# Attention with a second, small attention on one Trainium2 core: the masks of the token keys move ahead of most weight sums in the setup, and in the last batch the spreading of the probabilities and the bias move ahead

## The chip, the cores and the metric

The kernel runs on one core of one Trainium2 chip. The core has five engines that run side by side and meet through semaphores: the matrix engine (PE, which loads weights, PEld, and multiplies), VectorE (DVE), ScalarE (ACT), GpSimd (POOL) and SyncE (SP), which here issues nearly all DMAs. Each engine carries out its own instructions in the order in which the program gives them. The metric is the time on the device in microseconds (us); a profile is one execution recorded by the hardware.

## The reference

There are 16 batches of 100 rows of 640 (`hidden_states`), and for each batch 722 context rows of 384. The last four context rows are the tokens `ca`, the first 718 are `enc`. All is in float32, with eight heads of 80.

```python
query = hidden_states @ Wq;  keyt = enc @ Wk;  valt = enc @ Wv
hs = _mha(query, keyt, valt)
ca_q1 = jnp.einsum('btc,th->bch', ca, Wq_ca)[:, indices, :]   # 100 of 384 channels
ca_hs1 = _mha(ca_q1, residual, residual)
ca_q2 = ca_hs1 @ Wq
ca_hs2 = _mha(ca_q2, ca @ Wk_ca, ca @ Wv_ca)                  # four keys
out = (hs + ca_hs2) @ Wout + b_out + residual
```

`_mha` is softmax attention with the factor 80 to the power of -0.5.

## The kernel before, in words

The order of all instructions is written out by hand, engine by engine; nothing plans it. The kernel has a setup, a loop over the 16 batches, and a last projection.

**The products with the context.** The 3 x 2 blocks of the value product (three chunks of the 384 context channels, two halves of the 640 columns, three thirds of the context rows) are computed with 15 block products in place of 18, and those of the first four chunks of keys likewise. For that, sums of blocks of the weights are formed once (`weight_sums`, L511, one DVE instruction for each of twelve sums, at L531, for `wv_sb` and for `wk_sb` each), and sums of blocks of the context for each batch (`enc_sums`, L486, on POOL, L507). `weight_sums(engine, w, late, part)` goes through the list of twelve, of which `part` takes a slice; with `late` True or False it takes only those of the five forms (5, 7, 13, 3, 14) or only the others. Form 7 needs form 5, and 13 and 3 need 7. The block products of a batch and the copies and sums that move them out of PSUM are issued piece by piece by `vv.go(n)` (values, L439, moved at L410 and L412) and `kk.go(n)` (the next batch's keys, L470).

**The setup.** Seven idle products (L1257), then the first batch's keys (`first_keys`, L597). DVE forms the weight sums as the weights land. PE computes the keys of all tokens into `k2_ps` (L1289); DVE multiplies them by a mask of the heads, once for each of the five chunks of 128 columns (`k2T`, L1301; in the profile its tile bears the name `wq`, because it lies in a spare part of a tile of that name). With the masked keys PE computes `m` in five groups (`m_ps`, L1313), each of five products with the transposed Wq. DVE copies each group out (L1321), SP writes it to DRAM (L1325), and DVE forms one weight sum. POOL spreads `m` into `m2` for a batch (`keys`, L766, at L771); ACT copies Wq into place (L1272, L1280).

Then `Second`, the small attention of a batch: `products` (`y_ps`, L799; DVE reduces it into `g`, L808), `scores1` (`e1`, L834 and L841, for the first batch on DVE, for the others on POOL), `softmax1` (a maximum over blocks and its subtraction, L723 to L753 and L851, DVE), `exponentials1` (ACT, L854), and `softmax2` (`z_ps`, L861). `scores2` and `softmax3` give the probabilities of the four tokens: POOL writes them into `p2_in` (L900).

**A batch.** PE computes scores (`s_ps`, L660), ACT copies them into three tiles `st`, DVE takes the maximum over keys (L1399, L1408, and the class `Maximum`), subtracts it (`subtract`, L1387), and ACT takes the exponential (L1395). Then PE computes the rows' remaining columns and sums (`r_ps`, L1537) and the weighted values (`a_ps`, L1555). `divide` (L1025) takes the reciprocal of the sums on DVE and sends it through DRAM into `ratio` (SP, L1035 and L1038). `spread2` (L907) transposes the token probabilities on DVE (L910), writes them to DRAM with four DMAs (L913), copies them there in a wider layout (L918) and loads them back, spread over the partitions, with three more (L923, L927). `values2` (L929) then multiplies them by the token values on POOL, seven instructions (L937, L941), into `hs2`. `add_bias` (L1009) adds the bias to the loaded residual rows on POOL (L1015).

**The last batch** (L1491 to L1515) has no next batch to prepare. Two of its three subtractions are done by POOL, behind the first one on DVE. Behind them POOL has `values2` and then `add_bias`. DVE combines values, ratio and `hs2` for the last rows (`finish`, L1082, at L1086 and L1092, first chunk 4, then chunks 0 and 1, then 2 and 3), PE projects them (`project_last`, L1208, at L1219, in the order of chunks 4, 0, 1, and then 2 and 3), DVE adds the residual (L1228) and SP stores them (L1231).

Of the kernel before, what the change touches and what calls it, by code (L numbers as in the profile page):

```python
# [59 lines left out]
for h in range(NH):  # L60
    lo = h * D
    while lo < (h + 1) * D:
        c = lo // P
# [84 lines left out]
def kernel(  # L148
# [18 lines left out]
    nc = tc.nc  # L167
# [76 lines left out]
    def load_enc(b):  # L244
        enc = enc_tile(f"enc_{b}"), None
        for u, lo, hi in ((0, 0, 3), (1, 1, 3), (2, 0, 2)):
            at = A_RAW[u, lo]
            nc.sync.dma_start(
                out=enc[0][:, at : at + hi - lo],
                in_=enct[b][:, lo:hi, u * (KT - 1) : u * (KT - 1) + KT],  # L250
            )
        return enc

    def load_rest(b, enc):
        if b == 1:
            room = hsT_tile("rest_1").rearrange("p c s -> p (c s)")
            rest = room[:, : len(A_REST) * KT].rearrange("p (i k) -> p i k", k=KT)
        else:
            rest = rest_tile(f"rest_{b}")
        for (u, c), i in A_REST.items():  # L260
            nc.sync.dma_start(
                out=rest[:, i], in_=enct[b][:, c, u * (KT - 1) : u * (KT - 1) + KT]
            )
        return enc[0], rest
# [9 lines left out]
    wv_sb = const.tile([P, NF, H // 2], F32, name="wv_sb")  # L274
    wk_sb = const.tile([P, NF, 2, P], F32, name="wk_sb")
# [210 lines left out]
    def enc_sums(enc, part=slice(None)):  # L486

        at = lambda f: a_form(enc, f)
        raw = lambda u, c: a_raw(enc, u - 1, c - 1)
        sums = (  # L490
            (at(7), raw(2, 3), raw(3, 1), ALU.add),
            (at(11), raw(3, 2), raw(3, 3), ALU.add),
            (at(8), at(11), raw(2, 3), ALU.subtract),
            (at(10), raw(1, 3), at(11), ALU.subtract),
            (at(9), raw(2, 1), raw(2, 2), ALU.add),
            (at(2), raw(1, 1), at(9), ALU.subtract),
            (at(9), at(9), raw(3, 1), ALU.subtract),
            (at(5), raw(1, 1), raw(2, 1), ALU.subtract),
            (at(5), at(5), raw(2, 3), ALU.add),
            (at(11), raw(1, 3), raw(3, 3), ALU.subtract),  # L500
            (at(11), at(11), raw(3, 1), ALU.add),
            (at(4), at(2), at(10), ALU.add),
            (at(4), at(4), raw(1, 2), ALU.add),
        )
        begun = None
        for out, left, right, op in sums[part]:
            first = nc.gpsimd.tensor_tensor(out, left, right, op)  # L507
            begun = begun or first
        return begun

    def weight_sums(engine, w, late=None, part=slice(None)):  # L511

        at = lambda f: w[:, W_AT[f]]
        raw = lambda c, g: w[:, 2 * (c - 1) + g - 1]
        sums = (
            (0, raw(1, 2), raw(1, 1)),
            (11, raw(2, 2), raw(3, 2)),
            (12, raw(3, 2), raw(3, 1)),
            (5, raw(2, 2), raw(1, 2)),
            (7, raw(3, 2), at(5)),  # L520
            (13, raw(3, 1), at(7)),
            (1, raw(2, 1), raw(3, 1)),
            (3, raw(1, 1), at(7)),
            (6, raw(2, 1), raw(1, 1)),
            (10, raw(3, 1), raw(2, 2)),
            (2, raw(1, 1), raw(2, 2)),
            (14, raw(2, 1), raw(2, 2)),
        )
        for f, left, right in sums[part]:
            if late is None or late == (f in (5, 7, 13, 3, 14)):  # L530
                engine.tensor_tensor(at(f), left, right, ALU.subtract)  # L531
# [731 lines left out]
    nc.gpsimd.memset(most[96:, :], LOW)  # L1263
    nc.gpsimd.memset(e1[96:, :], LOW)
    weight_sums(nc.vector, wk_sb, False)
    weight_sums(nc.vector, wv_sb, part=slice(6))
    weight_sums(nc.vector, wk_sb, True)
    enc_sums(enc)

    for c in range(HC):  # L1270
        for u in range(2):
# [25 lines left out]
    for n, heads in enumerate(HEADS):  # L1297
        cols = len(heads) * B * T
        k2T.append(room[:, at : at + cols])
        at += cols  # L1300
        nc.vector.tensor_tensor(  # L1301
            k2T[n].rearrange("p (h k) -> p h k", h=len(heads)),
            k2_ps[:, n * B * T : (n + 1) * B * T]
            .unsqueeze(1)
            .to_broadcast([P, len(heads), B * T]),
            hmask[:, n, : len(heads)].unsqueeze(2).to_broadcast([P, len(heads), B * T]),
            ALU.mult,
        )
    enc_next = load_rest(1, load_enc(1))
    for c in range(HC):  # L1310
        m_ps = psum(f"m_ps_{c}")
        for n, heads in enumerate(HEADS):
            nc.tensor.matmul(  # L1313
                m_ps[:, heads[0] * B * T : (heads[-1] + 1) * B * T],
                wqt_sb[:, n, c * P : (c + 1) * P],
                k2T[n],
                start=(n == 0),
                stop=(n == HC - 1),
                skip_group_check=True,
            )  # L1320
        nc.vector.tensor_copy(  # L1321
            m_sb[c].rearrange("p (b h t) -> p h b t", h=NH, t=T),
            m_ps.rearrange("p (h b t) -> p h b t", h=NH, b=B),
        )
        nc.sync.dma_start(out=m_d[c], in_=m_sb[c])  # L1325
        weight_sums(nc.vector, wv_sb, part=slice(6 + c, 7 + c))
    weight_sums(nc.vector, wv_sb, part=slice(11, None))
    nc.sync.dma_start(out=wvca_sb, in_=wvca.rearrange("(c p) n -> p c n", p=P))
    second = Second(0, xT, ca_0)
    keys(load_m(0))  # L1330
# [37 lines left out]
    last, late, second_next = None, False, Second(1, xT)  # L1368
    for b in range(B):
        p = b // 2  # L1370
        e_in, now = enc, second
        enc, second = enc_next, second_next
        mine = Last(b)
# [51 lines left out]
        if b + 1 < B:  # L1425

            def both(n):
                vv.go(n)
                kk.go(n)

            if waiting:
                wait_for(enc_sums(enc, LATE_SUMS), seen)
            if waiting:
                second.scores1(tokens=range(T - 1))
            else:
                second.scores1(seen)
            store(seen)
            if last:
                last.load(seen)
            if b == B - 2:  # L1440
                again()
            if b + 2 < B:
                m_next = load_m(b + 2, seen)
            if b == 1:
                load_outputs(nc.sync.dma_start, wout_sb, wout)
            top.go(3)
            both(3)
            now.scores2()
            top.go(1)
            both(2)  # L1450
            top.go()
            both(2)
            now.softmax3()
            if waiting:
                second.scores1(tokens=range(T - 1, T))
            if b + 2 < B:
                keys(m_next)
            both(1)
            now.spread2()
            vv.go(2)  # L1460
            kk.go(1)
            subtract(0)
            exponential(0)
            vv.go(1)
            less = subtract(1)
            if last:
                last.place(less)
                if last.b in PAIRED:
                    last.row_sums()
                last.add_bias()  # L1470
            if b == B - 2:
                mine.load(seen)
            now.values2()
            if b == B - 2:
                mine.add_bias()
            vv.go(1)
            kk.go(2)
            exponential(1)
            vv.go(1)
            kk.go(2)  # L1480
            both(1)
            both(1)
            if b == 1:
                nc.gpsimd.dma_start(out=bias, in_=bout[0].partition_broadcast(P))
            second_next, enc_next = loads()
            subtract(2)
            exponential(2)
            last_keys(b + 1, enc)
            if b + 2 < B:
                enc_next = load_rest(b + 2, enc_next)  # L1490
        else:  # L1491
            last.place()
            mine.load(seen)
            top.go(3)
            vv.go(3)
            top.go(1)
            now.scores2()
            last.project_few(len(OC) - 2)
            last.project((0,), True, put=False)
            top.go()  # L1500
            now.softmax3()
            vv.go(2)
            less = subtract(0)
            exponential(0)
            wait_for(subtract(2, nc.gpsimd), less)
            subtract(1, nc.gpsimd)
            now.spread2()
            now.values2()
            mine.add_bias()
            vv.go(5)  # L1510
            exponential(2)
            vv.go(1)
            exponential(1)
            vv.go(4)
            last.put()  # L1515
        paired = last and last.b in PAIRED
        late = b % 2 == 0 and not paired
# [107 lines left out]
```

## Time and profile before

| | us |
|---|---|
| median of 3 runs | 927.84 (927.64 to 929.23) |
| the profiled execution | 925.61 |
| its span | 923.9 |
| mean granted PE clock | 0.998 |
| PE busy | 913.9 |
| DVE busy | 668.9 |
| POOL busy | 622.6 |
| ACT busy | 376.7 |

The profile's page gives the busy time of each engine; a row of its timeline is start, duration, engine, line, operation, the tile written and the tiles read, shapes and count, and in brackets how long the engine was idle before and whose work ended that. `PE` is the multiplying, `PEld` the loading of weights, and a letter q behind an engine's name its queue. The granted clock is the share of full speed at which PE ran.

### The profile page before, as it was taken

Reading aid. Unit: us, or ns where it says so; the run is one execution under the profiler, and the core shown is the slowest. Engines: PE = TensorE matmul, PEld = TensorE weight load, DVE = VectorE, ACT = ScalarE, POOL = GpSimd, SP = SyncE. Lnnn points to the kernel's source line nnn. Section 1 sums busy time; section 2 is a strip of 40 time slices with the busy share of each in tenths; the row PEclk is TensorE's granted clock in tenths of the full one; section 3 lists DMA queues with packets and bytes.
Section 4 is the critical chain, followed back from the end, with each engine's and each line's share of the span. In section 5 each row is a group of like instructions: output and inputs, shape, how many; then the busy total and the mean of one; then the engine's idle time right before and its main releaser. Section 6 shows DMA issues by size and latency. Waiting matters only on the chain.

```text
span 923.9 us, 26078 instructions
## 1 busy us (share of the span) xinstructions
PE 913.9 (99%) x11155; PEld 778.7 (84%) x11155; DVE 668.9 (72%) x1121; ACT 376.7 (41%) x654; POOL 622.6 (67%) x653
## 2 busy tenths in 40 slices
PE   9999999999999999999999999999999999999997
PEld 8988889797887979888798788988888888887965
DVE  4799695978639796675957759488782878729783
ACT  2253533444325443433434334344542435424441
POOL 9555787587946788476674756856695576945644
PEclk9999999999999999999999999999999999999999
DMA  9604251051402403140221403205140151401312
GB/s 293 207 13 131 52 131 39 15 133 34 109 12 57 118 15 100 43 131 12 70 74 43 131 13 87 65 5 135 41 109 11 35 141 34 110 12 46 84 45 71
DMA packets 68060, 69.50 MB, mean 75 GB/s; under 512 B 25192, under 2 KB 61352, under 8 KB 67944
## 3 DMA queue, kind: packets, MB, share of 16 engines
q1 hardware_dynamic: 67016, 66.97, 27.0%
q8 instruction: 88, 1.44, 0.6%
q10 hardware_dynamic: 464, 0.52, 0.2%
q0 software_dynamic: 464, 0.34, 0.2%
q14 instruction: 28, 0.23, 0.1%
HBM read 62.14 MB, written 8.94 MB: 77 GB/s over the span
## 4 chain that ended last, share of the span: by engine, by line
PE 92%; DMA 3%; DVE 2%; POOL 1%; ACT 1%; issue 0%; SPq 0%; POOLq 0%; ACTq 0%; DVEq 0%
PE s_ps L660 12%; PE v_psA L439 11%; PE v_psB L439 9%; PE k_psA L470 8%; PE q_ps L544 7%; PE a_ps L1555 7%; PE k_psB L470 7%; PE kT_ps L568 6%; PE r_ps L1537 4%; PE v_psC L439 3%; PE k_psC L470 3%; PE y_ps L799 2%; PE o_psy L1128 2%; PE v_psE L439 2%; PE v_psD L439 2%; PE k_psE L470 1%
## 5 line engine op out<-in xcount | busy, mean ns | idle before, releaser
L834 POOL TENSOR_TENSOR e<-ca,g 100x800 f32<-100x800 f32 x60 | 91.8, 1540 | 101.8 <-DVE most L1399 75.2
L439 PE MATMUL v_psA<-wv_sb,enc 128*120 128x320 f32 x384 | 119.5, 434 | 0.0
L507 POOL TENSOR_TENSOR enc<-enc 128x240 f32<-128x240 f32 x144 | 111.1, 781 | 8.0
L439 PE MATMUL v_psB<-wv_sb,enc 128*120 128x320 f32 x320 | 99.2, 432 | 0.0
L660 PE MATMUL s_ps<-qp,kT 32*120 32x100 f32 x3072 | 97.4, 263 | 0.0
L660 PEld LDWEIGHTS s_ps<-qp,kT 32*120 32x120 f32 x3072 | 94.7, 179 | 1.9
L841 POOL TENSOR_TENSOR e<-e,e 100x800 f32<-100x800 f32 x45 | 92.1, 2047 | 3.5
L439 PEld LDWEIGHTS v_psA<-wv_sb,enc 128*120 128x120 f32 x384 | 69.0, 183 | 24.7 <-DVE vs L410 0.9
L1387 DVE TENSOR_TENSOR st<-st,over 120x1600 f32<-120x1600 f32 x46 | 88.7, 1929 | 0.0
L470 PE MATMUL k_psA<-enc,wk_sb 128*128 128x240 f32 x360 | 87.6, 366 | 0.0
L470 PEld LDWEIGHTS k_psA<-enc,wk_sb 128*128 128x128 f32 x360 | 68.4, 190 | 17.1
L1399 DVE TENSOR_TENSOR most<-most,st 120x800 f32<-120x800 f32 x64 | 63.9, 998 | 23.3 <-ACT st L682 22.2
L439 PEld LDWEIGHTS v_psB<-wv_sb,enc 128*120 128x120 f32 x320 | 58.6, 183 | 23.4
L1395 ACT ACTIVATE st<-st 120x1600 f32<-120x1600 f32 x48 | 73.9, 1540 | 7.6 <-DVE st L1387 5.2
L470 PE MATMUL k_psB<-enc,wk_sb 128*128 128x240 f32 x300 | 73.0, 366 | 0.0
L1408 DVE TENSOR_TENSOR most<-st 120x800 f32<-120x800 f32 x16 | 16.5, 1032 | 75.9 <-ACT st L688 75.9
L1555 PE MATMUL a_ps<-st,vs 120*64 120x100 f32 (+1 forms) x1536 | 69.5, 250 | 0.0
L544 PE MATMUL q_ps<-xT,wq_sb 128*128 128x200 f32 x400 | 69.1, 332 | 0.0
L1555 PEld LDWEIGHTS a_ps<-st,vs 120*64 120x64 f32 (+1 forms) x1536 | 66.4, 137 | 2.7 <-issue 2.7
L544 PEld LDWEIGHTS q_ps<-xT,wq_sb 128*128 128x128 f32 x400 | 68.0, 190 | 0.2
L688 ACT COPY st<-s_ps 120x800 f32<-120x800 f32 x64 | 49.7, 829 | 43.4 <-PE s_ps L660 43.4
L412 ACT COPY vs<-v_psA 120x640 f32<-120x640 f32 x48 | 33.3, 693 | 83.7 <-PE v_psA L439 83.7
(183 smaller groups left out, 1893.1 us busy)
## 6 DMA issues: line engine op xcount, KB each, us to landing
pb<-p_d SPq DMA_DIRECT2D x32, 400.0 KB
enc<-in_enct SPq DMA_DIRECT2D x30, 240.0 KB
enc<-in_enct SPq DMA_DIRECT2D x15, 360.0 KB
xT<-in_xt SPq DMA_DIRECT2D x8, 500.0 KB
rest<-in_enct SPq DMA_DIRECT2D x31, 120.0 KB
xn<-in_x SPq DMA_DIRECT2D x11, 320.0 KB
wide_d<-p_d SPq DMA_DIRECT2D x16, 200.0 KB
pb<-wide_d SPq DMA_DIRECT2D x16, 200.0 KB
```

The source lines that it names most:

```text
L439: nc.tensor.matmul(at[0][j][:KN, : H // 2], a_form(self.enc, f)[:, j * KN : (j + 1) * KN], wv_sb[:, W_AT[f]], start=first, stop=last, skip ...
L470: nc.tensor.matmul(at[:, i * KT : (i + 1) * KT], wk_sb[:, W_AT[f], i], a_form(self.enc, f), start=(first and i == 0), stop=last, skip_grou ...
L507: first = nc.gpsimd.tensor_tensor(out, left, right, op)
L544: nc.tensor.matmul(q_ps[:, : 2 * S].rearrange("p (j s) -> p j s", j=2), wq_sb[:, c, n * P : (n + 1) * P], xT[:, :, c, :], start=(c == 0), ...
L568: nc.tensor.matmul(bank[:, i * KT : (i + 1) * KT], weights[c], a_raw(enc, u, c), start=(i == 0 and c == 0), stop=(c == CC - 1), skip_group ...
L660: nc.tensor.matmul(s_ps[bank][:n, 256 * a + lo : 256 * a + lo + rhs.shape[-1]], kT[rows, c, u, j * KN : (j + 1) * KN], rhs, start=bank not ...
L834: first = engine.tensor_tensor(to, self.ca[:, t, :].unsqueeze(1).to_broadcast([S, NH, S]), g[:, :, t].unsqueeze(2).to_broadcast([S, NH, S] ...
L841: engine.tensor_tensor(e, e, to, ALU.add)
L1387: return engine.tensor_tensor(st[i], st[i], top.over[:KN].unsqueeze(1).to_broadcast([KN, 2, ROWS]), ALU.subtract,)
L1395: nc.scalar.activation(st[i], st[i], AF.Exp, scale=SCALE)
L1399: most_now = nc.vector.tensor_tensor(most[:KN], most[:KN], st[i][:, u], ALU.max)
L1555: nc.tensor.matmul(wides[64 * e : 64 * e + 64, h // 2], slot(i, h, FIRST[e], 64), st[i // 2][: KEYS[i], i % 2, h * S : (h + 1) * S], start ...
```

## The change

In the setup DVE's order becomes: the seven early sums of `wk_sb`, four sums of `wv_sb` (six before), and then at once the five masks `k2T`. All five late sums of `wk_sb`, which stood ahead of the masks, and the last eight of `wv_sb` go into a list, in the order wk 5, 7, 13, 3, then eight of wv, then wk 14 (thirteen in all). Two of them are issued between the masks and m's loop, one behind each of m's five copies, and six behind the loop. (Before, one sum of wv stood behind each copy and one behind the loop.)

In the last batch `spread2` moves ahead of the second of the two block sums that stood ahead of it, and ahead of the three subtractions; `add_bias` moves ahead of `values2`. The number of instructions stays the same.

```diff
     weight_sums(nc.vector, wk_sb, False)
-    weight_sums(nc.vector, wv_sb, part=slice(6))
-    weight_sums(nc.vector, wk_sb, True)
+    weight_sums(nc.vector, wv_sb, part=slice(4))
     enc_sums(enc)
+    gaps = [(wk_sb, True, slice(k, k + 1)) for k in (3, 4, 5, 7)]
+    gaps += [(wv_sb, None, slice(k, k + 1)) for k in range(4, 12)]
+    gaps += [(wk_sb, True, slice(11, None))]
+
+    def fill(n):
+        for w, late, part in gaps[:n]:
+            weight_sums(nc.vector, w, late, part)
+        del gaps[:n]
...
+    fill(2)
     enc_next = load_rest(1, load_enc(1))
     for c in range(HC):
         m_ps = psum(f"m_ps_{c}")
...
         nc.sync.dma_start(out=m_d[c], in_=m_sb[c])
-        weight_sums(nc.vector, wv_sb, part=slice(6 + c, 7 + c))
-    weight_sums(nc.vector, wv_sb, part=slice(11, None))
+        fill(1)
+    fill(len(gaps))
...
             now.softmax3()
-            vv.go(2)
+            vv.go(1)
+            now.spread2()
+            vv.go(1)
             less = subtract(0)
             exponential(0)
             wait_for(subtract(2, nc.gpsimd), less)
             subtract(1, nc.gpsimd)
-            now.spread2()
+            mine.add_bias()
             now.values2()
-            mine.add_bias()
             vv.go(5)
```

## The prediction

> **What bounds the kernel now.** I read the page first, then every wait of the matrix engine, then the timeline around the two long ones, and the windows view for the clock.
>
> ```profile
> span 923.9 us, 26078 instructions
> PE 913.9 (99%) x11155; PEld 778.7 (84%) x11155; DVE 668.9 (72%) x1121; ACT 376.7 (41%) x654; POOL 622.6 (67%) x653
> ```
>
> PE is busy for 99% of the span, so time can only come out of PE's idle time or out of a slower PE clock. Its waits over the whole span, as total, count and longest (the two smallest left out):
>
> ```profile
> PE o_ps L1219 <- DVE spare L1092: 2.2, 1, 2.2
> PE m_ps L1313 <- DVE wq L1301: 1.8, 1, 1.8
> PE idle_ps L1257 <- DVE vaT L1254: 1.1, 1, 1.1
> PE z_ps L861 <- issue: 0.4, 1, 0.4
> PE k_ps L1289 <- ACT kT L631: 0.2, 1, 0.2
> PE z_ps L861 <- ACT e L854: 0.2, 1, 0.2
> ...
> ```
>
> The two largest are exactly where the diff works: m's products wait for the masked token keys (L1301), and the last projection waits for the last sum on DVE (L1092). Between them PE waits 0.6 us (two z_ps waits), so what is gained in the setup should arrive at the end.
>
> **Part 1, the setup.** Timeline of before (start, duration, engine, line):
>
> ```profile
> 17.85 5.01 DVE L531 TENSOR_TENSOR wv_sb<-wv_sb 128x320 f32<-128x320 f32 x6 [5.09 <-DMA wv_sb<-in_wv]
> 22.52 1.97 PE L1289 MATMUL k_ps<-beside,tokens 128*64 128x64 f32 x60 [0.24 <-ACT kT L631]
> 22.73 2.50 SPq L248 DMA_DIRECT2D enc<-in_enct  x3
> 22.78 3.27 DVE L531 TENSOR_TENSOR wk_sb<-wk_sb 128x256 f32<-128x256 f32 x5
> 25.98 1.20 DVE L1301 TENSOR_TENSOR wq<-k_ps,hmask 128x128 f32<-128x128 f32 x5
> 26.31 8.56 PE L1313 MATMUL m_ps<-wq,wout_sb 128*128 128x128 f32 x50 [1.82 <-DVE wq L1301]
> 29.37 0.29 ACT L1280 COPY wq_sb<-wq 128x128 f32<-128x128 f32 x1
> 32.27 0.69 DVE L1321 COPY m<-m_ps 128x512 f32<-128x512 f32 x1 [0.23 <-PE m_ps L1313]
> ...
> 34.91 0.69 DVE L1321 COPY m<-m_ps 128x512 f32<-128x512 f32 x1 [0.23 <-PE m_ps L1313]
> 35.51 0.98 DVE L531 TENSOR_TENSOR wv_sb<-wv_sb 128x320 f32<-128x320 f32 x2
> 37.56 0.26 DVE L808 TENSOR_REDUCE g<-y_ps 100x32 f32<-100x96 f32 x1 [1.07 <-PE y_ps L799]
> 53.92 0.99 DVE L851 TENSOR_TENSOR e<-e,over 100x800 f32<-100x800 f32 x1
> 56.56 0.90 ACT L854 ACTIVATE e<-e 100x800 f32<-100x800 f32 x1
> ```
>
> PE has the token keys at 22.52 + 1.97 = 24.49. DVE masks them only at 25.98, because eleven weight sums stand ahead of the masks. The change leaves four of these (17.85 + 4 x 5.01 / 6 = 21.2), so DVE reaches the masks long before 24.49 and waits for PE instead. Nothing is queued behind that wait that anyone needs earlier. The mask of chunk n needs only chunk n's columns: m's first product started 0.33 after the first of five masks began, so slices are followed one by one on this side, and I take it that they are on the other. Then m starts right behind the token keys, at about 24.5, and the 1.82 us go. The other end: if the first mask waits for all token keys, m starts 0.33 after 24.49 and 1.5 go. I take 1.8. No weight sum is added or removed, only moved.
>
> There is a second cost behind this gap. Windows of before (us, busy of PE, PEld, DVE, ACT, POOL, then the granted clock, DMA share, GB/s):
>
> ```profile
> 23.45:26.87 3.42, 1.59 (x40) 1.46 (x37) 3.28 (x9) 1.97 (x7) 1.57 (x2) 1.00 1.06 363
> 26.87:30.28 3.41, 3.41 (x15) 3.41 (x15) 1.40 (x4) 2.52 (x9) 0.47 (x1) 0.50 1.02 298
> 30.28:33.70 3.42, 3.42 (x28) 3.42 (x27) 2.29 (x5) 0.00 (x0) 1.00 (x2) 1.00 0.47 175
> 910.84:914.25 3.41, 1.57 (x38) 1.37 (x32) 1.30 (x1) 0.00 (x0) 3.33 (x3) 1.00 0.27 81
> ```
>
> Right after the stretch with the gap, PE was granted half its clock for 3.41 us: 15 matmuls in place of 28. That cost 3.41 x 0.5 = 1.7 us. The copies confirm it: the copies at 32.27 and 34.91 stand two groups of m apart, so a group takes 1.32; five would be 6.6, and m took 8.56, 1.96 more. The page's forty slices hide this. I take it that the gap caused it and that it goes too: 1.7. The other end is 0, since the last row, a stretch of the tail with as little PE work, was not followed by a low clock.
>
> The Trainium skill, page "TensorE: Matmul & The Clock Gate", Part 1 on the clock gate, says that the clock halves after about one whole idle window of roughly 3.4 us and that the windows run freely. The length of the low stretch agrees; the cause does not, for the gap was 1.82. By that rule this gap could not have lowered the clock, so the low stretch would have another cause, and could come again; that is the first rival.
>
> What is late next? Shift the setup by 3.5. The query weights are copied by 29.37 + 0.29 = 29.66, and the first queries then start at 26.31 + 8.56 - 3.5 = 31.4: covered. SP's issue at 22.73 waited for the landing of the transposed Wq that m reads (SP's waits name that transfer), so m's weights are there before 24.5. Two wk sums now stand between masks and m's first copy, 2 x 3.27 / 5 = 1.3 at most against 1.32 of PE for one group; within the loop a copy and a sum (0.69 + 0.49) fit into 1.32. Behind the last copy, six sums stand in place of two: 6 x 0.49 = 2.9, from 34.91 + 0.69 - 3.5 = 32.1 to 35.0. The first batch's g (L808) could start at 34.06 and so is 0.9 late against its shifted place. From g to the end of L851 took 54.91 - 37.56 = 17.35, which gives 52.4; ACT takes e up at 56.56 - 3.5 = 53.1. The 0.7 between hide it: I cost it at nothing. With sums as slow as the six beside POOL's (0.84 each, 5.0), g would start at 37.1, L851 end at 54.5, and z_ps wait 1.4 more: the other end.
>
> **Part 2, the last batch.** Timeline of before, with two rows of the batch ahead:
>
> ```profile
> 872.58 1.29 SPq L1038 DMA_DIRECT2D ratio<-inv_d  x2
> ...
> 876.35 0.27 POOL L1077 TENSOR_TENSOR hsT<-hsT,ratio 128x40 f32<-128x40 f32 x1 [1.90 <-DMA ratio<-inv_d]
> ...
> 890.84 0.24 POOL L900 TENSOR_TENSOR p_in<-e,sm 100x32 f32<-100x32 f32 x1 [8.90 <-DVE sm L899]
> 891.49 0.82 DVE L410 TENSOR_TENSOR vs<-v_psB,vs 120x640 f32<-120x640 f32 x1
> 893.96 0.20 DVE L910 STREAM_TRANSPOSE p2t<-p_in 128x32 f32<-128x32 f32 x1
> 894.19 7.14 POOL L1387 TENSOR_TENSOR st<-st,over 120x1600 f32<-120x1600 f32 x2 [3.11 <-DVE p2t L910]
> 904.95 1.03 POOL L937 TENSOR_TENSOR hs<-pb,vaT 128x500 f32<-128x500 f32 x1 [3.62 <-DMA pb<-wide_d]
> 908.06 4.35 PE L1555 MATMUL a_ps<-st,vs 120*64 120x100 f32 x96
> 908.58 1.25 SPq L1038 DMA_DIRECT2D ratio<-inv_d  x2
> 911.67 1.24 POOL L941 TENSOR_TENSOR hs<-hs,pb 128x500 f32<-128x500 f32 x1
> 912.87 1.53 POOL L1015 TENSOR_TENSOR spare<-spare,bias 128x640 f32<-128x640 f32 x1
> 912.95 1.57 DVE L1092 TENSOR_TENSOR spare<-spare,hs 128x100 f32<-128x100 f32 x1 [3.55 <-POOL hs L941]
> 914.45 0.35 DVE L1086 TENSOR_TENSOR spare<-a_ps,ratio 128x200 f32<-128x200 f32 x1
> 914.58 5.65 PE L1219 MATMUL o_ps<-wout_sb,spare 128*128 128x480 f32 x20 [2.17 <-DVE spare L1092]
> 914.83 0.37 DVE L1092 TENSOR_TENSOR spare<-spare,hs 128x200 f32<-128x200 f32 x1
> ```
>
> The transpose of the probabilities (L910) moves ahead of the B block's sum, to about 891.45: its input is ready at 890.84 + 0.24 = 891.08. Its eight DMAs move with it, 2.5 earlier; SP has nothing else queued there. The probabilities land at 904.9 - 2.5 = 902.4. DVE's subtraction behind it slips by under 0.1. POOL subtracts until 901.4, then adds the bias, which moved ahead (1.53, to 902.9): this, not the transfer, starts the values now, 2.05 before 904.95, and they end at 912.91 - 2.05 = 910.9. DVE's first L1092 follows at once, and without the bias beside it, which ran through its 1.57.
>
> PE's own work now comes last: a_ps ends at 908.06 + 4.35 = 912.41, and the last projection's first chunk can follow directly, so the 2.17 go. The next chunks need L1086 and L1092 on a_ps (0.35 and 0.37), ready about 913.3, while PE's first chunk runs to 912.41 + 5.65 / 5 = 913.5. The ratio must have landed by 912.6: the batch ahead took 876.35 - 872.58 = 3.8 from issue to use, which gives 912.35 here, just in time. If it landed only as DVE used it before (914.45), 0.5 would be left. I take 2.1, by the row of the batch ahead.
>
> **The sum.** 1.8 + 1.7 + 2.1 = 5.6 us. The profiled execution took 925.61 in all (span 923.9), which gives 920.0. The runs' median is 927.84, 2.2 above it; against that I predict 922.2.
>
> **The rivals.**
> - *The low clock stays* (its cause is not the gap, or the timed runs do not have it): 1.8 + 2.1 = 3.9, 923.9. For it: the tail's gap without a low clock. Against it: the low stretch begins where the stretch with the gap ends.
> - *The late sums take PE's place as releaser*: e comes 1.4 late at z_ps, and a new gap there lowers the clock again (1.7): 922.2 + 3.1 = 925.3. For it: six sums ahead of g. Against it: the two sums there took 0.49 each beside POOL's work.
> - *The ratio decides the tail*: 1.6 of it is lost, 923.8.
> - *The head does nothing*, m's start being held by another input: 927.84 - 2.1 = 925.7. The row at 22.73 speaks against it.
> - *Slower*: the transpose now stands ahead of DVE's subtraction and waits for POOL's p_in. Each us of that wait delays subtraction, POOL's 7.14, the last exponential and PE one for one. It outweighs the rest from 5.6 us on and shows as slower from 7.5 (929.7). Against it: p_in ended 0.3 before DVE gets there.
>
> **How the numbers follow.** Forecast 0.52, low clock stays 0.2, late sums 0.1, ratio 0.07, head nothing 0.05, slower 0.06. A measurement can tell 0.2%, 1.9 us, here; the fourth rival lies at that bound and counts as same, the cases ahead of it are faster by more: 0.89 faster, 0.05 same, 0.06 slower. The range runs from 920.4 (the timed runs, 2.2 above the profiled one, may have paid a second low stretch of 1.7 at the tail's gap, which would go as well) to 925.5, past the late sums.
>
> **What would show it.** Right: m starts within 0.4 of the token keys' end, the clock stays at 1.00 through m, POOL's bias lies ahead of the values, they start near 903 less the shift, and o_ps L1219 follows a_ps with no wait. Wrong: z_ps waiting over 1 us for e, L1086 waiting for the ratio, L910 waiting for p_in, or a stretch at half clock elsewhere in the first 60 us.

## The result, and the profile after

| | before | after |
|---|---|---|
| median of the runs on one chip, us | 927.32 (925.99 to 929.23) | 921.09 (920.74 to 921.48) |
| ratio | | 0.9933 (95%: 0.992 to 0.9946) |
| the profiled execution, us | 925.61 | 921.04 |
| its span, us | 923.9 | 919.3 |

The changed kernel is 6.2 us faster by the medians; the two profiled executions differ by 4.57. One execution of the kernel before, beside the last four experiments, took 1047.76 us at a granted clock of 0.851 and is left out of every comparison. The head of the page of after, and its waits of PE (total, count, longest in us):

```profile
span 919.3 us, 26076 instructions
PE 912.0 (99%) x11155; PEld 776.6 (84%) x11155; DVE 665.5 (72%) x1121; ACT 376.6 (41%) x654; POOL 620.6 (68%) x653
```

```profile
PE idle_ps L1257 <- DVE vaT L1254: 1.1, 1, 1.1
PE w_ps L589 <- DMA kT<-in_wkt: 0.8, 2, 0.5
PE m_ps L1321 <- DVE wq L1308: 0.5, 1, 0.5
PE kT_ps L620 <- DVE wk_sb L592: 0.3, 1, 0.3
...
PE z_ps L861 <- ACT e L854: 0.2, 1, 0.2
...
```

The two waits at which the change aimed stood at the head of this list before. That of `o_ps` L1219 is gone, and that of `m_ps` (L1313 before, L1321 now) has shrunk from 1.8 to 0.5. New in the list are only 0.8 and 0.3 at the first keys (`w_ps`, `kT_ps`), which lie in the first 11 us, ahead of the change. The timeline of after in the setup (start, duration, engine, line, operation, in brackets the idle time before and its releaser):

```profile
23.07 1.97 PE L1296 MATMUL k_ps<-beside,tokens 128*64 128x64 f32 x60 [0.24 <-ACT kT L631]
25.16 1.21 DVE L1308 TENSOR_TENSOR wq<-k_ps,hmask 128x128 f32<-128x128 f32 x5 [4.19 <-PE k_ps L1296]
25.50 6.91 PE L1321 MATMUL m_ps<-wq,wout_sb 128*128 128x128 f32 x50 [0.46 <-DVE wq L1308]
33.05 2.83 DVE L531 TENSOR_TENSOR wv_sb<-wv_sb 128x320 f32<-128x320 f32 x6
36.24 0.24 DVE L808 TENSOR_REDUCE g<-y_ps 100x32 f32<-100x96 f32 x1
52.48 0.99 DVE L851 TENSOR_TENSOR e<-e,over 100x800 f32<-100x800 f32 x1
54.10 0.91 ACT L854 ACTIVATE e<-e 100x800 f32<-100x800 f32 x1
55.05 0.75 PE L861 MATMUL z_ps<-y,e 100*32 100x33 f32 x64 [0.21 <-ACT e L854]
```

DVE now waits 4.19 for PE in place of the other way round. It starts the masks when all token keys are done (23.07 + 1.97 = 25.04, masks at 25.16), and PE's idle time there is 0.46 in place of 1.82. `m` takes 6.91 in place of 8.56. The windows view of after shows why (busy time of PE, PEld, DVE, ACT and POOL, then the granted clock, the DMA share and GB/s):

```profile
22.48:25.90 3.42, 2.71 (x65) 2.23 (x64) 0.74 (x4) 1.31 (x4) 1.83 (x3) 1.00 1.04 395
25.90:29.31 3.41, 3.41 (x27) 3.41 (x27) 3.08 (x9) 3.22 (x12) 0.46 (x2) 1.00 1.07 328
```

The clock stays at 1.00 behind the gap; 27 matmuls stand where 15 stood before. The timeline of the last batch:

```profile
888.02 0.24 POOL L900 TENSOR_TENSOR p_in<-e,sm 100x32 f32<-100x32 f32 x1 [11.17 <-DVE sm L899]
888.86 0.20 DVE L910 STREAM_TRANSPOSE p2t<-p_in 128x32 f32<-128x32 f32 x1
899.00 1.54 POOL L1015 TENSOR_TENSOR spare<-spare,bias 128x640 f32<-128x640 f32 x1
900.50 1.04 POOL L937 TENSOR_TENSOR hs<-pb,vaT 128x500 f32<-128x500 f32 x1
905.76 4.35 PE L1564 MATMUL a_ps<-st,vs 120*64 120x100 f32 x96
908.53 0.27 DVE L1092 TENSOR_TENSOR spare<-spare,hs 128x100 f32<-128x100 f32 x1 [1.25 <-POOL hs L941]
910.04 5.65 PE L1219 MATMUL o_ps<-wout_sb,spare 128*128 128x480 f32 x20
910.15 0.37 DVE L1086 TENSOR_TENSOR spare<-a_ps,ratio 128x200 f32<-128x200 f32 x1 [1.36 <-PE a_ps L1564]
```

POOL's bias now lies ahead of the values and they follow it directly. DVE's sum (L1092) ends at 908.80, 1.3 before `a_ps` does (905.76 + 4.35 = 910.11), and takes 0.27 in place of 1.57 because no bias runs beside it. The last projection starts with no idle time before it. DVE's L1086 waited for `a_ps`, and not for the ratio.

So the 4.57 between the two profiled executions divide, to within 0.03, into 1.36 (the gap ahead of m), 1.65 (m itself) and 2.08 (from m's end, 34.87 before and 32.41 after, to the last projection's start, 914.58 and 910.04), less 0.55, by which the token keys ended later in this execution (25.04 against 24.49).

### The profile page after: what moved, and what is told of

It reads as the page before. It is cut to its first block, busy times and chain, and to the rows that moved or that the text cites. A ratio compares the mean times of both kernels' runs of the same rounds, so it can differ in the third digit from the quotient of the medians.

```text
span 919.3 us, 26076 instructions
## 1 busy us (share of the span) xinstructions
PE 912.0 (99%) x11155; PEld 776.6 (84%) x11155; DVE 665.5 (72%) x1121; ACT 376.6 (41%) x654; POOL 620.6 (68%) x653
## 4 chain that ended last, share of the span: by engine, by line
PE 97%; DMA 1%; POOL 1%; ACT 0%; DVE 0%; issue 0%; ACTq 0%; SPq 0%; DVEq 0%; POOLq 0%
PE s_ps L660 12%; PE v_psA L439 11%; PE v_psB L439 9%; PE k_psA L470 8%; PE a_ps L1564 7%; PE q_ps L544 7%; PE k_psB L470 7%; PE kT_ps L568 6%; PE r_ps L1546 4%; PE v_psC L439 4%; PE k_psC L470 3%; PE y_ps L799 2%; PE v_psD L439 2%; PE o_psy L1128 2%; PE v_psE L439 2%; PE k_psE L470 1%
## 5 line engine op out<-in xcount | busy, mean ns | idle before, releaser
L507 POOL TENSOR_TENSOR enc<-enc 128x240 f32<-128x240 f32 x144 | 108.7, 765 | 8.0
```

## The experiments

Each comparison below has its own runs of the kernel before, on the same chip: 926.77 for the first four, 927.12 for the next four, 926.5 for the last four. The first question is how the gain divides.

**The setup's change alone** (after, with the last batch's order put back):

```diff
             now.softmax3()
-            vv.go(1)
-            now.spread2()
-            vv.go(1)
+            vv.go(2)
             less = subtract(0)
...
-            mine.add_bias()
+            now.spread2()
             now.values2()
+            mine.add_bias()
```

> The setup's part alone (the last batch as before). Theory: the gap ahead of m shrinks from 1.82 to 0.46 us and the low clock behind it (8.56 against 6.91 us for m) goes with it: 1.4 + 1.65 = 3.0 us faster, m at clock 1.00, the last projection still waiting 2.2 us for L1092. Rival (the low clock is not the gap's doing): only 1.4 us faster, and a stretch at half clock somewhere in the first 40 us.

Measured: 924.93, ratio 0.998 (0.9962 to 0.9998), 1.8 us where 3.0 were expected. Its timeline, the last line from the tail:

```profile
24.80 1.97 PE L1296 MATMUL k_ps<-beside,tokens 128*64 128x64 f32 x60 [0.24 <-ACT kT L631]
27.23 6.91 PE L1321 MATMUL m_ps<-wq,wout_sb 128*128 128x128 f32 x50 [0.46 <-DVE wq L1308]
...
914.54 7.34 PE L1219 MATMUL o_ps<-wout_sb,spare 128*128 128x480 f32 x20 [2.38 <-DVE spare L1092]
```

In the setup m waits 0.46 and takes 6.91, as in after. But the token keys end late in this execution (26.77), and the next experiment shows that m then waits 0.46 with the old order too. What the new order does is seen where the keys end early: m waits 0.46 in after (keys at 25.04) and in the run with six more sums below (24.53), against 1.82 to 2.58 in four traces with the old order (24.49 to 24.66). In the tail, the projection behind the gap takes 7.34 in place of 5.65: in this execution the stretch of low clock stands there.

**The last batch's change alone** (before, with the other half of the diff):

```diff
             now.softmax3()
-            vv.go(2)
+            vv.go(1)
+            now.spread2()
+            vv.go(1)
             less = subtract(0)
...
-            now.spread2()
-            now.values2()
             mine.add_bias()
+            now.values2()
```

> The last batch's part alone (the setup as before). Theory: the 2.17 us wait of the last projection goes and nothing takes its place: 2.2 us faster, the gap of 1.8 us and the half clock in the setup as before. Rival (the gain in the tail hangs on the setup, or the ratio's landing decides): 0.5 us or less.

Measured: 922.77, ratio 0.9963 (0.995 to 0.9977): 4.0 us, where 2.2 were expected. The parts add up (1.8 + 4.0 = 5.8), but the larger one is the tail's. In the profile the projection starts without a wait; the head shows something else:

```profile
24.45 1.97 PE L1289 MATMUL k_ps<-beside,tokens 128*64 128x64 f32 x60 [0.24 <-ACT kT L631]
26.88 6.91 PE L1313 MATMUL m_ps<-wq,wout_sb 128*128 128x128 f32 x50 [0.46 <-DVE wq L1301]
```

The setup here is the old one, and yet m waited only 0.46: in this execution the token keys ended at 26.42, not 24.49, so the masks were not late. How late PE comes to the token keys differs between executions, and where it is late the setup's change has little idle time to remove. The traces show where the time goes. The same four products of the first keys, in before and in this run:

```profile
7.18 0.97 PE L620 MATMUL kT_ps<-enc,wk_sb 128*128 128x240 f32 x4
8.04 1.81 PE L620 MATMUL kT_ps<-enc,wk_sb 128*128 128x240 f32 x4
```

They take nearly twice as long here. The three traces with 1.81 in this row (this run, the setup alone, and the second profile of after) are the three in which the token keys end at 26.4 to 26.8. So in these executions PE comes up to speed later; what decides that was not tested.

**Which of the tail's two moves does it?** Only the spreading ahead (the bias stays behind the values), and only the bias ahead:

```diff
             now.softmax3()
-            vv.go(2)
+            vv.go(1)
+            now.spread2()
+            vv.go(1)
...
-            now.spread2()
             now.values2()
             mine.add_bias()
```

> Only the spreading moved ahead in the last batch; the bias stays behind the values. Theory: values start when the probabilities land, about 2.5 us earlier than before, so they end about 2 us ahead of a_ps; the bias then still runs beside the first L1092 and makes it slow (1.57 us in place of 0.27), but both end ahead of a_ps: 2.2 us faster, the whole gain of the tail, the move of the bias worth nothing. Rival (both moves are needed): 1.0 to 1.5 us faster, L1092's end still the releaser of the last projection.

```diff
             now.spread2()
-            now.values2()
             mine.add_bias()
+            now.values2()
```

> Only the bias moved ahead of the values; the spreading stays behind the subtractions. Theory: the values start with the landing as before, the bias fits into POOL's wait of 3.6 us ahead of them; the first L1092 takes 0.27 us in place of 1.57 since nothing runs beside it on POOL: 1.3 us faster, the last projection still waiting 0.9 us. Rival (the slow L1092 is not POOL's doing): no change.

Measured: the spreading alone 922.94, ratio 0.9962 (0.9949 to 0.9976); the bias alone 924.65, ratio 0.9977 (0.9963 to 0.9992); that is 3.8 and 2.1 us, where 2.2 and 1.3 were expected. Timelines of the first and of the second:

```profile
903.22 1.04 POOL L937 TENSOR_TENSOR hs<-pb,vaT 128x500 f32<-128x500 f32 x1 [1.36 <-DMA pb<-wide_d]
908.59 4.34 PE L1556 MATMUL a_ps<-st,vs 120*64 120x100 f32 x96
911.16 1.54 POOL L1015 TENSOR_TENSOR spare<-spare,bias 128x640 f32<-128x640 f32 x1
911.24 1.58 DVE L1092 TENSOR_TENSOR spare<-spare,hs 128x100 f32<-128x100 f32 x1 [1.25 <-POOL hs L941]
912.87 5.65 PE L1219 MATMUL o_ps<-wout_sb,spare 128*128 128x480 f32 x20
```

```profile
904.75 1.03 POOL L937 TENSOR_TENSOR hs<-pb,vaT 128x500 f32<-128x500 f32 x1 [2.10 <-DMA pb<-wide_d]
912.73 0.26 DVE L1092 TENSOR_TENSOR spare<-spare,hs 128x100 f32<-128x100 f32 x1 [3.54 <-POOL hs L941]
913.05 5.65 PE L1219 MATMUL o_ps<-wout_sb,spare 128*128 128x480 f32 x20 [0.84 <-DVE spare L1092]
```

With the spreading alone DVE's sum still runs beside the bias and takes 1.58, but it ends (912.82) just before `a_ps` does (912.93), and the projection does not wait. It is worth as much as both together (922.94 and 922.77). With the bias alone the values still wait for the probabilities, and only the 1.3 that L1092 no longer spends beside the bias are saved in the trace; the rest of the 2.1 goes with the low clock (the six runs with a mean clock of 1.000 have a median of 924.1, 1.3 under such runs of the kernel before). Either move would have helped; they do not add up, and the second was already covered by PE's own work.

**Does the gap lower the clock?** Six products of zeros, behind the token keys of the kernel before, were to fill most of its gap:

```diff
+    for _ in range(6):
+        nc.tensor.matmul(
+            k2_ps[:, HC * B * T : HC * B * T + P],
+            idle,
+            idle,
+            start=True,
+            stop=True,
+            skip_group_check=True,
+        )
     k2T, at = [], 0
```

> The kernel before, with six products of zeros (128x128, about 1.3 us) put behind the token keys, into free columns, so that PE is busy in the gap ahead of m while the masks are as late as before. Theory (the gap causes the low clock): m takes 6.9 us in place of 8.56 though it starts no earlier: 1.65 us faster. Rival (the low clock has another cause, as the Trainium skill's rule of one whole idle window in the page TensorE: Matmul & The Clock Gate would have it for a gap of 1.8 us): m takes 8.5 us again, no change.

Measured: 926.53, ratio 0.9989 (0.9975 to 1.0003), which decides nothing: m waited 1.29 and took 6.91, but the next kernel shows that m takes 6.91 in some executions of the kernel before as well. That one is **the kernel before itself**, run again:

> The kernel before itself, to see the granted clock of each of its runs. The gap between its times (925.99 to 929.23 us) is wider than the changed kernel's (920.74 to 921.48). Theory: its runs differ in the number of stretches at half clock (one stretch of 3.41 us costs 1.7 us and shows as a mean clock of 0.998, two as 0.996), according to where the two gaps of 1.8 and 2.2 us fall: slower runs have the lower clock. Rival: the clock is the same in all of them, and the spread has another source.

Measured: 927.45, ratio 0.9997 (0.998 to 1.0013). Its timeline, and its windows at the end:

```profile
27.05 6.91 PE L1313 MATMUL m_ps<-wq,wout_sb 128*128 128x128 f32 x50 [2.53 <-DVE wq L1301]
...
914.52 8.69 PE L1219 MATMUL o_ps<-wout_sb,spare 128*128 128x480 f32 x20 [3.00 <-DVE spare L1092]
```

```profile
910.46:913.87 3.41, 1.06 (x26) 0.86 (x21) 0.98 (x1) 0.00 (x0) 3.33 (x4) 1.00 0.13 44
913.87:917.28 3.41, 2.76 (x5) 1.71 (x6) 1.88 (x5) 0.00 (x0) 0.47 (x1) 0.50 0.00 0
917.28:920.69 3.41, 3.41 (x7) 1.69 (x6) 0.00 (x0) 0.00 (x0) 0.00 (x0) 0.50 0.00 0
```

The same kernel, and the picture is turned round: a longer gap in the head (2.53) without a low clock, and in the tail a gap of 3.00 with two stretches of it. So the two gaps of the kernel before are two places where the clock can fall, and executions differ in whether it falls behind the one, the other, both or neither.

**The gap shortened from the other side:** two of the sums of `wk_sb` moved behind the masks, and nothing else.

```diff
-    weight_sums(nc.vector, wk_sb, True)
+    weight_sums(nc.vector, wk_sb, True, slice(6))
...
+    weight_sums(nc.vector, wk_sb, True, slice(6, None))
     enc_next = load_rest(1, load_enc(1))
```

> The kernel before with two of the late sums of wk (forms 3 and 14) moved from ahead of the masks to behind them: the gap ahead of m is about 1.1 us in place of 1.8. Theory (the clock falls only when a gap takes about half of a stretch of 3.41 us): 0.7 us of gap and the 1.65 us of low clock go, 2.3 us faster. Rival (any gap of a us behind the small token products lowers it): 0.7 us faster, m still at 8.5 us.

Measured: 926.29, ratio 0.9989 (0.9974 to 1.0005), not to be told from no change. The timeline shows that the gap did not become what was meant:

```profile
19.43 5.10 DVE L531 TENSOR_TENSOR wv_sb<-wv_sb 128x320 f32<-128x320 f32 x6 [6.69 <-DMA wv_sb<-in_wv]
26.60 6.91 PE L1314 MATMUL m_ps<-wq,wout_sb 128*128 128x128 f32 x50 [2.01 <-DVE wq L1301]
```

The weights of the values landed later in this execution (the sums begin at 19.43, in the profile of before at 17.85), and with six sums of them still ahead of the masks these came as late as before. The run therefore doesn't show what a shorter gap would bring. It shows that the landing of a DMA decides over the masks as long as six sums that wait for it stand ahead of them.

**What do the late sums cost once their cover is gone?** Six more sums of `wv_sb` behind m's loop of after (sums are formed in place, so the second forming changes the values that follow):

```diff
     fill(len(gaps))
+    weight_sums(nc.vector, wv_sb, part=slice(4, 10))
```

> The changed kernel with six sums of wv formed a second time behind m's loop, so that DVE reaches the first batch's g 2.9 us later. Theory: the slack of the first batch's e ahead of the exponential, 0.6 us in the changed kernel's trace (L851 ends at 53.47, L854 starts at 54.10), is used up and PE waits 2.3 us more at z_ps: 2.3 us slower than the changed kernel, 4.0 if the new gap lowers the clock. Rival (that path has room by ACT's and DVE's other work): less than 0.5 us slower.

Measured: 927.08, ratio 0.9997 (0.9986 to 1.0009), some 6 us more than after, where 2.3 were expected, or 4.0 with a low clock. Its timeline:

```profile
35.73 4.76 DVE L531 TENSOR_TENSOR wv_sb<-wv_sb 128x320 f32<-128x320 f32 x6
40.42 0.24 DVE L808 TENSOR_REDUCE g<-y_ps 100x32 f32<-100x96 f32 x1
57.82 0.87 ACT L854 ACTIVATE e<-e 100x800 f32<-100x800 f32 x1 [4.09 <-DVE e L851]
58.74 0.76 PE L861 MATMUL z_ps<-y,e 100*32 100x33 f32 x64 [4.41 <-ACT e L854]
```

The place was right: the first batch's `g` is late, then the exponential, then `z_ps`, where PE waits 4.41. The price was not: the last six sums take 0.79 each, beside POOL's sums of the context, where the six of after took 0.47 each (2.83 / 6). PE's wait is 4.2 longer than in after, and in this profile half clock begins at 59.36, behind the wait, for another 1.7. All ten runs had a mean clock of 0.998 or less.

**How long must the gap be?** This was tried in after, where no wait of PE is longer than 1.1: the first mask is formed 5 times, and 11 times, in place of once.

```diff
-        nc.vector.tensor_tensor(
...
+        for _ in range(1 if n else 5):
+            nc.vector.tensor_tensor(
...
```

> The changed kernel with the first mask formed five times, so that the gap ahead of m grows from 0.46 to about 1.35 us. Theory (the clock falls when PE was idle for over half of a free-running stretch of 3.41 us, which 1.35 never reaches): no run at 0.998, and 0.9 us over x10_after. Rival (any gap over one us may lower it): some runs at 0.998, about 1.7 us over the others.

> The same with the first mask formed eleven times: the gap ahead of m is about 2.65 us. Theory (over half of a stretch of 3.41 us): a gap of 2.65 us leaves the clock alone only if the stretches divide it so that neither has over 1.7, in (3.41 - 2.65) / 3.41 = 22% of the runs; about three runs in four are at 0.998, 1.7 us over the others, and the fastest lie 2.2 us over x10_after. Rival (it takes a whole idle stretch of 3.41 us, as the Trainium skill has it in the page TensorE: Matmul & The Clock Gate): all runs at 1.000.

After itself ran beside them:

> The changed kernel itself, beside the others of this call. Theory: with no gap over 0.5 us, every run is at a mean clock of 1.000 or 0.999, and its times lie close together, about 6 us under the kernel before. Rival (the low clock comes by itself): some runs at 0.998.

Measured: after 921.26, ratio 0.9941 (0.9922 to 0.9959); five masks 922.10, 0.9947 (0.9927 to 0.9966); eleven masks 925.86, 0.9994 (0.9979 to 1.0009). The timelines of the two, and the windows of the second:

```profile
26.39 6.91 PE L1322 MATMUL m_ps<-wq,wout_sb 128*128 128x128 f32 x50 [1.76 <-DVE wq L1309]
```

```profile
28.31 8.29 PE L1322 MATMUL m_ps<-wq,wout_sb 128*128 128x128 f32 x50 [3.71 <-DVE wq L1309]
```

```profile
24.46:27.87 3.41, 0.14 (x6) 0.00 (x0) 2.85 (x10) 1.10 (x4) 0.22 (x1) 1.00 1.05 330
27.87:31.28 3.41, 2.97 (x12) 2.97 (x13) 2.04 (x9) 3.24 (x12) 0.00 (x0) 0.50 0.74 237
```

A mask more cost 0.3, not the 0.2 reckoned with, so the gaps came out longer than meant. With 1.76 none of six runs had a mean clock below 0.999, and the time rose by 0.8, which the intervals do not tell from no change. With 3.71 all twelve had 0.998 or less, and it rose by 4.6, of which the gap itself is 3.71 - 0.46 = 3.25 and the slower m 8.29 - 6.91 = 1.38. The Trainium skill, page "TensorE: Matmul & The Clock Gate", Part 1, says that the clock halves after at least one idle window of about 3.4 us, and that the windows run freely. The length of the low stretch agrees (3.41). The condition does not. By an estimate from that rule, a gap of 3.71 holds a whole window in about one run of eleven ((3.71 - 3.41) / 3.41), if windows fall anywhere; in this run the clock fell in twelve of twelve, and the gap of 1.82 in the profile of before was well short of a window. The measurement decides.

**Is there more to gain at the head?** The token keys were computed ahead of the last third of the first batch's keys, in free columns of the same PSUM banks, and the masks put ahead of the sums of `wv_sb`:

```diff
         for c, chunks in ((0, (0, 1)), (0, (2, 3)), (1, range(4)), (2, range(4))):
+            if c == 2:
...
+                token_keys()
...
     weight_sums(nc.vector, wk_sb, False)
+    k2T, at = [], 0
+    for n, heads in enumerate(HEADS):
...
     weight_sums(nc.vector, wv_sb, part=slice(4))
```

> The changed kernel with the products of the token keys put ahead of the last third of the first batch's key products, into free columns of their banks, and the masks ahead of all sums of wv. Theory: the masks wait for the last of the token keys' products whatever chunk they need, so a gap of 0.46 us is left ahead of m, and 0.24 us ahead of the token keys; with other products between, both go: 0.7 us faster than the changed kernel (x10_after, same chip), no wait of m's products. Rival (the next input, the transposed Wq or a bank, is late too): less than 0.3 us.

Measured: 922.10, ratio 0.9949 (0.993 to 0.9967), 0.8 more than after beside it, and not the 0.7 less that was expected; the intervals do not tell the two kernels apart. Its timeline:

```profile
24.91 1.22 DVE L1294 TENSOR_TENSOR wq<-kT_ps,hmask 128x128 f32<-128x128 f32 x5 [12.25 <-ACT kT L654]
25.25 6.91 PE L1334 MATMUL m_ps<-wq,wout_sb 128*128 128x128 f32 x50 [0.90 <-DVE wq L1294]
32.90 2.49 DVE L531 TENSOR_TENSOR wv_sb<-wv_sb 128x320 f32<-128x320 f32 x6
33.06 2.81 POOL L794 TENSOR_TENSOR m<-m,hmask 128x64 f32<-128x64 f32 x1 [0.48 <-DVE m L1342]
35.94 0.41 PE L822 MATMUL y_ps<-m,xT 128*100 128x96 f32 x2 [1.29 <-POOL m L794]
```

The token keys' own products were done by 19.3, but the masks started only at 24.91, and the bracket names ACT's copies of the first keys out of the same banks: the wait followed something other than the columns read. Whether the other products or ACT's reading held it was not separated. So m started no earlier behind the last key products, and a new cost appeared: one of POOL's spreadings of `m` took 2.81 (in after the one at this place took 0.47), as long as DVE's row of sums beside it, and PE waited 1.29 for it. No version tried was faster than the changed kernel.

## Why the prediction was right

Predicted were 922.2 (920.4 to 925.5) and faster; measured were 921.09. Of the 1.1 between them 0.5 is the kernel before, which has a median of 927.32 here and had 927.84 in the three runs from which the forecast was made; 0.6 is the gain, 6.2 in place of 5.6.

The mean granted clock of each timed run divides the gain further. Over 924 us one stretch of 3.41 at half clock lowers the mean by 3.41 x 0.5 / 924 = 0.0018, so the mean counts the stretches. For the kernel before, in the runs that went with the second four experiments:

| mean granted clock | stretches | runs | median, us |
|---|---|---|---|
| 1.000 | 0 | 12 | 925.49 |
| 0.998 | 1 | 16 | 927.35 |
| 0.996 | 2 | 4 | 929.05 |
| 0.994 | 3 | 3 | 930.50 |

Every run of after was at 0.999 or 1.000, in both sets of six. Runs at 0.999 or above show the idle time without the clock. Beside the first four experiments these are: before 925.4 (12 runs), the setup alone 924.1 (4), the tail alone 922.7 (7). So the gaps give 1.3 in the setup and 2.7 in the tail. Both together were run beside the kernel before, with all clocks on record, in the last four: 925.2 (6 runs) and 921.3 (6), which is 3.9 of 5.3, and leaves 1.4 for the clock. (A run without a low stretch may also be one with a short gap, so the split is not exact. The clocks of the kernel before in the runs of the result, where the gain was 6.2, are not on record.)

Where the clock is lost can be counted in the same way. Beside the first four experiments the kernel before has 25 low stretches in 31 runs. With the tail's gap alone left (the setup alone) there are low stretches in 6 of 10 runs; with the tail's gap gone or cut to 0.84 (the other three) in 10 of 30, and with both changes in none of 12. Each gap lowers the clock on its own: 0.6 and 0.33 a run come to 0.93, against 25 / 31 = 0.81.

- **"I take 1.8" for the idle time ahead of m: mis-sized.** It was 1.36 in the profile and 1.3 in the timed runs. The prediction let the first mask wait only for its chunk's columns; it waits for all token keys, which was named as the other end (1.5). So m started 0.46 behind the keys, just outside the 0.4 that was named as a sign of being right. The early masks of the last experiment waited for more than their own columns as well.
- **"I take it that the gap caused it and that it goes too: 1.7": right in the profile (1.65), mostly wrong as a price for the timed runs.** A gap there can lower the clock, as the eleven masks show. But it does so in about 10 of 30 runs, which makes 0.33 x 1.7 = 0.6 and not 1.7. So the setup alone gave 1.8 in place of 3.5.
- **"I take 2.1" for the tail: right in the profile (2.08), too small for the timed runs (2.7).** In four other executions with the old tail the gap was 2.29 to 3.00, not 2.17. The timed runs paid a low stretch there too, in 6 of 10, or 0.6 x 1.7 = 1.0; the sum put nothing for it, and the prediction had it only as the low end of the range.
- **The bias "starts the values now": it does** (899.00 + 1.54, values at 900.50), but the time was the same with the bias behind the values. The step "and without the bias beside it" bought nothing that `a_ps` did not cover.
- **PE's `a_ps` comes last: right.** The ratio was not late, nor did the transpose (L910) keep the subtraction waiting for POOL's `p_in`.
- **The late sums "at nothing": right.** L851 ended at 53.47, ACT took `e` up at 54.10, and `z_ps` waited 0.2. The 0.6 left are what the prediction called 0.7; with six sums more it was gone.
- **The rival "the low clock stays"** fell: after has no low stretch in any run, and lengthening the gap ahead of m to 3.71 brings it back in all.

The mechanisms named were there, but that the sum of 5.6 came so near was in part luck. Its setup's part was too large (3.5 against 1.8 measured alone), its tail's part too small (2.1 against 4.0), and the 1.7 for the clock is near what the two gaps lost together, though it was all charged to the first.

## What to carry to other kernels

An idle stretch of PE can cost more than its length, and one profile does not show how often: here two gaps of two to three microseconds each lowered the clock in some executions and not in others, and the profile of the kernel before shows only one of them. Compare the mean granted clock of all timed runs, not the clock of one trace. And when an engine's order has two things ahead of a late result, move the one that waits for a transfer first; whether the second still matters is decided by what the next engine has left to do.

## What the runs showed of the hardware

- **When the clock falls.** The recorded changes of the clock within a trace lie whole multiples of 3.41 us apart, so they mark stretches that run on through the execution. If a stretch is taken to end 0.4 us ahead of the possible change, PE's idle time within one stretch separates all cases of the fourteen traces (in brackets the whole gap):

  | clock behind the stretch | PE's idle time within it, us |
  |---|---|
  | halved | 1.82 (1.82), 1.85 (2.08), 1.95 (3.00), 2.10 (2.58), 2.28 (2.29), 2.38 (2.38), 2.87 (3.71), 3.20 (4.41) |
  | stays full | 1.76 (1.76), 1.60 (2.01), 1.58 (2.61), 1.53 (2.17), 1.48 (2.53); all others 1.29 or less |

  The length of the whole gap does not separate them: 2.61 left the clock alone and 1.82 lowered it, since a gap that lies across the border of two stretches is split. A gap of 3.71 has at least 1.85 in one stretch however it is split, and lowered the clock in all runs. The offset was fitted (0.25 to 0.45 do as well), so this is a pattern, not a proof, and it does not cover how long the clock stays low: behind the gap of 3.00 it stayed so for two stretches.
- **One instruction shut out for the length of a row.** POOL's spreading took 2.81 in place of 0.47 beside DVE's unbroken row of sums, and ended 0.48 behind it (32.90 + 2.49 = 35.39, 33.06 + 2.81 = 35.87). The Trainium skill, page "SBUF — State Buffer", section "Who interferes with whom", says that DVE and POOL take turns at a shared port by an exclusive lock. The trace agrees in kind; that an instruction can be shut out for five sums in a row is what this row adds. It need not be: in after the same instruction took 0.47 beside the same sums. The milder form is DVE's L1092, 0.27 alone and 1.57 beside POOL's bias.
- **The wait on a PSUM tile followed the whole tile.** The first mask began at 25.16 in after, behind the last product into `k_ps` (25.04) and not behind those of its own chunk; with the token keys in the first keys' banks it came 5.6 behind them (24.91 against 19.3). On the other side m's products followed the masks, which lie in SBUF, one by one: the first began at 25.50, the five masks ended at 26.37. Whether the chip asks for this or the semaphores of this program was not separated.
- **Executions differ in the setup by more than the setup's gain.** Where the first keys' four products took 1.81 in place of 0.97, the token keys ended at 26.4 to 26.8 in place of 24.5 to 25.0 (25.9 with the six products of zeros behind them).
